# A batch of layer 3 moved ahead of a folding, and the last unit of a scan summed part by part

## The chip, the cores and the metric

The kernel runs on one core of one Trainium2 chip. The metric is the device time of one execution in microseconds (us). The five engines run their own instruction queues side by side: PE (matrix products, from SBUF into PSUM), DVE and POOL (elementwise work), ACT (functions and copies) and SP, which here issues the DMAs.

## The reference

Four layers run one after the other over 8 images of 192 channels and 64 x 64 pixels, all in f32.

- Layer 0: normalisation, a gate branch, a 3x3 depthwise convolution, then a selective scan in four directions, normalised, gated, weighted by channel and added to the input.
- Layer 1: a mixing layer with no recurrence.
- Layer 2: a selective scan again, and a normalisation.
- Layer 3: windows of the image, in three layouts, go through a small attention and a 3x3 depthwise convolution, and are folded back.

The scan, with h a state of 16 values for each channel, and cut to its core:

```python
def step(h, inp):
    dt_t, B_t, C_t, x_t = inp
    h = h * jnp.exp(dt_t[..., None] * A[None]) + (dt_t * x_t)[..., None] * B_t[:, :, None, :]
    return (h, jnp.einsum('bkcn,bkn->bkc', h, C_t))
```

Layer 3, with the three layouts (number of windows along a side, step, window side): (4, 16, 16), (8, 8, 8) and (12, 5, 9). The windows of the third overlap:

```python
xc = _conv1x1(x, w1, b1)
for nw in WINDOWS:
    ...
    u4 = u3.reshape(-1, C, k, k)
    a = _se(_conv1x1(u4, w2, b2), wse1, wse2) + _dwconv3x3(u4, wpos, bpos)
    ...
    folded = jnp.zeros((N, C, H, W), xc.dtype).at[:, :, hidx, widx].add(p)
    out_list.append(folded / cnt[None, None, :, :])
out = _conv1x1(jnp.concatenate(out_list, axis=1) + x, w3, b3)
```

The `reshape` to `u4` mixes pixels and channels, so each batch passes through DRAM on its way in and out.

## The kernel before

For each image the program runs `scan_layer` (layer 0's scan), `layer0_out`, `layer1`, `put_sequences`, `scan_layer` again (layer 2's scan) and `between`. There are so 16 scan layers in an execution. `between` mixes two generators: `behind`, the rest of this image (end of layer 2, and layer 3), and `ahead`, the start of the next image. For the last image it holds `behind` alone.

**The scan.** A scan layer has 48 units: two directions, eight chunks of 512 positions, three groups of 128 channels. The order on every engine is written out by hand (`manual_schedule`): the loop over `k` is the unit, the loop over `j` its eight steps. A unit's state tile `da` is 128 partitions by 4 parts (`NB`) by 16 states (`NS`) by 128 positions (`SB`). Per unit:

- ACT writes the decay into `da` (L244). PE fills the input `u` (L287). DVE scans two times per part (L308).
- `times_c` multiplies each part by C on POOL (L319, 128x2048), as soon as its two scans are done, in the next step `j`. POOL then adds the last states onto others (L322), four of them in the first two parts and three in the other two, so that 12 (or 13) states are left.
- `add_up` sums the states on PE, with matmuls by the identity that accumulate in the PSUM tile `py`: one matmul of 512 columns for each of 12 states over all four parts (L337), and one of 256 columns for the 13th state of the last two (L342). They are queued in the list `to_add` at step 2 of the next unit and drawn off a few at a time.
- `finish` adds the sum to the rest in `yo` on DVE (L352, L356) and stores it (L357). `load_y` loads, in the second direction, what the first one left (L328).

The loop runs for two turns beyond the last unit, so that its sum and its `finish` have a place. The pools of the next stage take the scan's memory when its last store has landed.

**Layer 3.** `behind` works on four batches of windows: two halves of the third layout (`first`, `second`), the first layout (`third`) and the second (`fourth`). `gates` loads a batch (L897), sets it into a padded tile and works out the gate. `convolve` makes the 3x3 taps in groups (six for each half of the third layout, four for each of the others). In a group PE makes four taps (L939), ACT one (L951), POOL the gated input (L945) and its sum with ACT's tap (L954), DVE the last four (L957) and the sum of all (L960). At the end the batch is stored to DRAM (L966). `move_windows` loads a layout back (L860): the third layout `p2` into tile `t1`, later the first two, `p01`, into the same tile `t1`.

Folding adds windows onto the image: the third layout on DVE (one half of the partitions, ten ops) and POOL (the other half, eight ops) at L991, after the accumulator was zeroed on POOL (L985), then two scalings of the overlaps on DVE (L999, L1002); the first two layouts on DVE and POOL in turn (L1011). The output follows (L1020 to L1028).

In `between` the order in which the program is written gives the priorities, but the order on each engine is drawn up by a planner when the program is built, so instructions can pass others that aren't ready.

Of the kernel before, what the change touches and what calls it, by code (L numbers as in the profile page):

```python
# [9 lines left out]
ALU = mybir.AluOpType  # L10
# [11 lines left out]
NS = 16  # L22
SB = 128
NB = Q // SB
# [16 lines left out]
def tile_net(ctx: ExitStack, tc: tile.TileContext, a: dict, out: bass.AP):  # L41
    nc = tc.nc
# [5 lines left out]
    ident = cst.tile([P, P], F32, name="ident")  # L48
# [50 lines left out]
    def scan_layer():  # L99
# [5 lines left out]
        with (  # L105
# [13 lines left out]
            NP = 12  # L119
            units = [  # L120
                (d, i, i if d == 0 else nck - 1 - i, v)
                for d in range(2) for i in range(nck) for v in range(3)
            ]
            vt, xd, cdr, dg = {}, {}, {}, {}
            dts, dtx, dtt, das, cts, us, py, yo = {}, {}, {}, {}, {}, {}, {}, {}

# [189 lines left out]

            def times_c(k, g):
                h = das[k][:, NB - 1 - g if units[k][0] else g]
                nc.gpsimd.tensor_tensor(h, h, cts.pop((k, g)), ALU.mult)  # L319
                n = NS - NP if g < 2 else NS - NP - 1  # L320
                to = h[:, NP - n : NP]
                nc.gpsimd.tensor_tensor(to, to, h[:, NS - n : NS], ALU.add)  # L322
# [9 lines left out]
            def add_up(count):  # L332

                for k, n in to_add[:count]:
                    if n == 0:
                        py[k] = sp.tile([P, Q], F32, tag="py", name="py")
                    nc.tensor.matmul(  # L337
                        py[k], ident, das[k][:, :, n, :], start=(n == 0), stop=(n == NP - 1)
                    )
                    if n == 8:  # L340
                        s = slice(0, NB // 2) if units[k][0] else slice(NB // 2, NB)
                        nc.tensor.matmul(  # L342
                            py[k][:, s.start * SB : s.stop * SB], ident, das[k][:, s, NP, :],
                            start=False, stop=False,
                        )
                del to_add[:count]

            def finish(k):
                d, i, c, v = units[k]
                p, y = py.pop(k), yo.pop(k)  # L350
                if d == 0:
                    nc.vector.scalar_tensor_tensor(  # L352
                        y, vt[k // 3][:, v, :], skip[:, v : v + 1], p, ALU.mult, ALU.add
                    )
                else:
                    nc.vector.tensor_tensor(y, y, p, ALU.add)  # L356
                nc.sync.dma_start(out=(ys if d else yp)[v][:, c * Q : (c + 1) * Q], in_=y)  # L357

            nu, nm = len(units), len(units) // 3


            SUM = ((1, 0, 1, 2, 0, 2, 1, 2), (2, 2, 1, 1, 1, 2, 2, 2), (2, 1, 1, 2, 2, 2, 2, 2))
# [2 lines left out]
            def has(k):  # L365
                return 0 <= k < nu
# [24 lines left out]
                    fill(0, 0)  # L391
            for r in range(2):
                diagonals_b(0, 1, r)
            for k in range(nu + 2):
                m, v = divmod(k, 3)
                ahead = 0 <= m + 1 < nm
                for j in range(8):
                    if v == 1 and j == 3 and 0 <= m + 2 < nm:
                        load_v(m + 2)
                    if has(k):  # L400
                        scan(k, j)
                    if j == 7:
                        if has(k + 1):
                            cut(k + 1)
                        if has(k):
                            keep(k)
                    if j % 2 == 0:
                        kk, g = (k, j // 2 - 1) if j else (k - 1, 3)
                        if has(kk):
                            times_c(kk, g)  # L410
                        if has((4 * kk + g + 3) // 4):
                            load_c(*divmod(4 * kk + g + 3, 4))
                    if j == 5 and has(k + 2):
                        steps_c(k + 2)
                    kk, jj = (k, j + 1) if j < 7 else (k + 1, 0)
                    if has(kk):
                        fill(kk, jj)
                    if j == 2:
                        if has(k - 2):
                            finish(k - 2)  # L420
                        if has(k - 1):
                            load_y(k - 1)
                        if has(k + 1):
                            turn(k + 1)
                    if ahead and (v, j) == (0, 4):

                        steps_a(k + 3)
                        steps_a(k + 4)
                    if ahead and v == 1 and j == 1:

                        steps_b(k + 2)
                        steps_a(k + 4)
                        steps_b(k + 3)
                        steps_b(k + 4)
                    if v == 0 and ahead:
                        if j == 0:
                            project_a(m + 1)
                        if j == 1:
                            project_b(m + 1)
                    if v > 0 and ahead:  # L440
                        if j == (5, 1)[v - 1]:
                            diagonals_a(m + 1, v - 1)
                        if j >= 6:
                            diagonals_b(m + 1, v - 1, j - 6)
                    if j == 2 and has(k - 1):
                        to_add += [(k - 1, n) for n in range(NP)]
                    add_up(SUM[v][j])
                    if has(k + 1) and j in DECAY:
                        decay(k + 1, *DECAY[j])

# [343 lines left out]
    def behind(b, pool, wk, psp, table):  # L794
# [55 lines left out]
        def move_windows(i, t, dram, store):  # L850
            if i < 2:
                pairs = [(t[half(i)], dram[i])]
            else:
                pairs = [(t[half(0)], dram[2][:, 0 : 45 * 144])]
                pairs += [(t[half(1)][:, 0 : 36 * 144], dram[2][:, 45 * 144 :])]
            for s, d in pairs:
                if store:
                    nc.sync.dma_start(out=d, in_=s)
                else:
                    nc.sync.dma_start(out=s, in_=d)  # L860
# [71 lines left out]
        def convolve(k, kk, mh, per, u4, pad, gate, to):  # L932
            for g in range(0, mh, per):
                ms = slice(g, g + per)
                ps = wide_("pw")[:, 0]
                tap = [divmod(t, 3) for t in range(9)]
                tap = [pad[:, g // per, dy : dy + k, dx : dx + k, :] for dy, dx in tap]
                for t in range(PE_TAPS):
                    nc.tensor.matmul(  # L939
                        ps[:, : per * kk], taps[:, t, :], tap[t],  # L940
                        start=(t == 0), stop=(t == PE_TAPS - 1),
                    )
                acc = wk.tile([P, Q], F32, tag="acc", name="acc")[:, : per * kk]
                turned = u4[:, ms, :].rearrange("p m j -> p j m")
                nc.gpsimd.tensor_tensor(  # L945
                    acc.rearrange("p (j m) -> p j m", m=per), turned,
                    gate[:, ms].unsqueeze(1).to_broadcast([P, kk, per]), ALU.mult,
                )
                tap = [t.rearrange("p r q m -> p r (q m)") for t in tap]
                term = wk.tile([P, Q], F32, tag="term", name="term")[:, : per * kk]  # L950
                nc.scalar.mul(  # L951
                    term.rearrange("p (r x) -> p r x", r=k), tap[PE_TAPS], pos[:, PE_TAPS : PE_TAPS + 1]
                )
                nc.gpsimd.tensor_tensor(acc, acc, term, ALU.add)  # L954
                rows = ps[:, : per * kk].rearrange("p (r x) -> p r x", r=k)
                for t in range(PE_TAPS + 1, 9):
                    nc.vector.scalar_tensor_tensor(  # L957
                        rows, tap[t], pos[:, t : t + 1], rows, ALU.mult, ALU.add
                    )
                nc.vector.scalar_tensor_tensor(  # L960
                    turned, ps[:, : per * kk].rearrange("p (j m) -> p j m", m=per), bpos,
                    acc.rearrange("p (j m) -> p j m", m=per), ALU.add, ALU.add,
                )
                yield "conv"
            for h, (af, m0) in enumerate(to):
                nc.sync.dma_start(out=af[:, m0 : m0 + mh, :], in_=u4[half(h)])  # L966
# [12 lines left out]
        fourth = gates(1, 0, 1, "t0", "t3")  # L979
        yield "gates"  # L980
        yield from convolve(*third)


        acc = room("t2", size["t2"])[:, 0:T]
# [16 lines left out]
        both = both.rearrange("p h (g r) -> p h g r", r=s)[:, :, :, 0 : k - s]  # L1001
        nc.vector.tensor_scalar_mul(both, both, 0.5)  # L1002
        p01 = room("t1", size["t1"])[:, 0:T]
        move_windows(0, p01, a3, False)
        yield from convolve(*fourth)
        move_windows(1, p01, a3, False)
        for i in range(2):
            nw, s, k = WINDOWS[i]
            for ki in range(k):
# [318 lines left out]
```

## Time and profile before

| | us |
|---|---|
| median of 3 runs | 25658.43 |
| lowest and highest | 25636.73, 25665.45 |
| the profiled execution | 25655.22 |
| its span | 25653.4 |

| engine | busy us | share of the span | instructions |
|---|---|---|---|
| PE (matmul) | 23083.9 | 90% | 173960 |
| DVE | 20611.1 | 80% | 21237 |
| POOL | 19165.2 | 75% | 7452 |
| ACT | 14171.8 | 55% | 23120 |

The mean granted clock of PE was 0.938 of full speed. "Busy" is an average over stages that have different limits. What counts for a change in one stage is what ends last there, so the shares above say little by themselves: the chain of waits and the timeline of the stage do. Times in those views are microseconds from the start of the span; "x7" means seven instructions merged into one row, and "[2.28 <-POOL da L319]" that the engine stood idle 2.28 us until POOL's instruction of line 319 was done.

### The profile page before, as it was taken

The page shows a single profiled execution, that of the slowest core. Times are in us where ns is not written, and L with a number is a line of the kernel's source. Part 1 is how long each engine was busy: PE and PEld are TensorE (multiplying, and loading weights), DVE is VectorE, ACT ScalarE, POOL GpSimd, SP SyncE. Part 2 cuts the span into 40 slices and gives each one's busy share as a digit, 9 for nine tenths or more (in the row PEclk, how much of TensorE's full clock was granted, in tenths as well). Part 3 has the DMA queues.
Part 4 walks back from the last instruction along what each step waited for, and adds up shares of the span by engine and source line. Part 5 has one row for each costly group of instructions (what it writes and reads, how often), then busy time and mean ns, then how long its engine had stood idle before and what let it go on. Part 6 is the DMA issues. An engine that isn't in the chain of part 4 may idle for free.

```text
span 25653.4 us, 431230 instructions
## 1 busy us (share of the span) xinstructions
PE 23083.9 (90%) x173960; PEld 12032.7 (47%) x173960; DVE 20611.1 (80%) x21237; ACT 14171.8 (55%) x23120; POOL 19165.2 (75%) x7452
## 2 busy tenths in 40 slices
PE   9989889898898988989889898898989989799896
PEld 4535345353453534535345353453535535355452
DVE  7969789697896968969689696886968879688795
ACT  5646456464564645646456464555645556455563
POOL 7939589395893958939589395894958949589495
PEclk9989999899998999989999899998999989899898
DMA  5636556365563655636556365563656646566364
GB/s 168 207 115 203 144 174 206 115 202 144 172 206 115 204 145 170 206 116 203 142 174 206 115 203 140 178 202 120 204 134 181 200 122 204 132 186 202 118 204 115
DMA packets 1204797, 4293.85 MB, mean 167 GB/s; under 512 B 360224, under 2 KB 419456, under 8 KB 804480
## 3 DMA queue, kind: packets, MB, share of 16 engines
q1 hardware_dynamic: 1202816, 4266.25, 56.5%
q8 instruction: 1388, 22.74, 0.4%
q14 instruction: 593, 4.86, 0.1%
HBM read 3810.55 MB, written 450.72 MB: 166 GB/s over the span
## 4 chain that ended last, share of the span: by engine, by line
POOL 37%; PE 12%; DVE 7%; ACT 3%; issue 3%; DMA 2%; SPq 0%; POOLq 0%; DVEq 0%; ACTq 0%
POOL da L319 28%; POOL da L322 6%; PE py L337 3%; POOL dtx L221 2%; PE u L287 2%; DVE da L308 2%; PE pa L501 1%; ACT da L244 1%; DVE pwc L957 1%; PE pa L504 1%; DVE t L991 1%; DMA a<-t 1%; DMA t<-u 0%; PE paa L501 0%; PE pac L501 0%
## 5 line engine op out<-in xcount | busy, mean ns | idle before, releaser
L308 DVE TENSOR_TENSOR_SCAN da<-da,u 128x1024 f32<-128x1024 f32 x6144 | 14041.7, 2286 | 324.1 <-ACT da L254 37.4
L319 POOL TENSOR_TENSOR da<-da,ct 128x2048 f32<-128x2048 f32 x3072 | 13925.0, 4533 | 330.7 <-DVE tmp L303 309.2
L337 PE MATMUL py<-da,ident 128*128 128x512 f32 x18432 | 9491.8, 627 | 542.2 <-POOL da L319 442.9
L287 PEld LDWEIGHTS u<-dg,dtt 32*128 32x128 f32 x131072 | 5942.5, 163 | 4597.8 <-issue 4309.1
L244 ACT ACTIVATE da<-dt,neg_a 128x512 f32<-128x512 f32 (+1 forms) x12544 | 7662.8, 699 | 16.3
L287 PE MATMUL u<-dg,dtt 32*128 32x128 f32 x131072 | 7232.6, 283 | 115.6 <-DVE da L308 48.6
L337 PEld LDWEIGHTS py<-da,ident 128*128 128x128 f32 x18432 | 3120.3, 191 | 3144.0 <-issue 2226.5
L322 POOL TENSOR_TENSOR da<-da 128x512 f32<-128x512 f32 (+1 forms) x3072 | 3484.2, 1134 | 240.9
L221 POOL TENSOR_TENSOR dtx<-dt,vt 128x512 f32<-128x512 f32 x768 | 978.2, 1275 | 3311.3 <-ACT dt L217 3245.6
L231 ACT COPY dtt<-misc 128x512 f32<-128x512 f32 x768 | 449.4, 585 | 3336.9 <-PE misc L229 3336.9
L305 DVE TENSOR_TENSOR u<-u,tmp 128x8 f32<-128x8 f32 x5952 | 1009.0, 170 | 1089.2 <-PE u L287 867.1
L234 ACT COPY dtt<-misc 32x512 f32<-32x512 f32 x3008 | 1732.2, 576 | 45.4
L196 DVE TENSOR_TENSOR dg<-msk,misc 128x1024 f32<-128x1024 f32 x1024 | 1222.9, 1197 | 440.1 <-DMA vt<-vs 277.8
L160 ACT ACTIVATE xd<-misc,msk 128x512 f32<-128x512 f32 x256 | 175.6, 686 | 1789.9 <-PE misc L156 1789.9
L217 ACT ACTIVATE dt<-misc 128x512 f32<-128x512 f32 x768 | 430.7, 595 | 1104.1 <-PE misc L213 1095.2
L945 POOL TENSOR_TENSOR acc<-u,gate 128x486 f32<-128x486 f32 (+1 forms) x80 | 108.3, 1358 | 966.7 <-DVE u L960 690.7
L939 PE MATMUL pwc<-t,l3taps 128*128 128x486 f32 (+1 forms) x1280 | 598.5, 617 | 233.4 <-DVE t L960 213.4
L901 POOL MEMSET t<- 128x4356 f32 (+2 forms) x32 | 100.3, 3135 | 936.9 <-DVE t L875 914.5
L229 PE MATMUL misc<-ident,dtx 128*128 128x128 f32 x3072 | 595.4, 318 | 0.0
L186 PE MATMUL misc<-ident,xd 16*128 16x16 f32 x4096 | 565.5, 266 | 25.6 <-DVE dg L196 25.6
L186 PEld LDWEIGHTS misc<-ident,xd 16*128 16x128 f32 x4096 | 528.1, 210 | 94.6 <-issue 93.1
L951 ACT ACTIVATE term<-t,l3p 128x486 f32<-128x486 f32 (+1 forms) x160 | 114.1, 713 | 826.4 <-POOL acc L954 826.4
(286 smaller groups left out, 18279.6 us busy)
## 6 DMA issues: line engine op xcount, KB each, us to landing
ct<-cd SPq DMA_DIRECT2D x2048, 1024.0 KB
ct<-cd SPq DMA_DIRECT2D x2048, 512.0 KB
vt<-vs SPq DMA_DIRECT2D x768, 256.0 KB
yp<-yo SPq DMA_DIRECT2D x384, 256.0 KB
yo<-yp SPq DMA_DIRECT2D x384, 256.0 KB
ys<-yo SPq DMA_DIRECT2D x384, 256.0 KB
yt<-ys SPq DMA_DIRECT2D x96, 512.0 KB
t<-ys SPq DMA_DIRECT2D x96, 512.0 KB
```

The costliest lines, as they stand in the source:

```text
L186: nc.tensor.transpose(pt[:, i * NS : (i + 1) * NS], xd[m][rows, cols], ident[rows, rows])
L196: nc.vector.tensor_tensor(dg[m, o][:, at], msk[:, 0:32].unsqueeze(1).unsqueeze(1).to_broadcast(shape), bts[m, o][:, at, r * 8 : r * 8 + 8] ...
L221: nc.gpsimd.tensor_tensor(dtx[k], dts[k], vt[k // 3][:, units[k][3], :], ALU.mult)
L234: (nc.scalar.copy if k else nc.vector.tensor_copy)(dtt[k][q * 32 : (q + 1) * 32, 1], pt[r * 32 : (r + 1) * 32])
L244: nc.scalar.activation(das[k][:, s, n, :], dts[k].rearrange("p (s t) -> p s t", t=SB)[:, s], AF.Exp, scale=neg_a[:, v, d, n : n + 1],)
L287: nc.tensor.matmul(u[ch, r * 4 : r * 4 + 4, e::4], dtt[k][rows, r, e, ch], dg[k // 3, o][rows, r * 4 + e, n], start=True, stop=True,)
L305: nc.vector.tensor_tensor(head, head, tmps[k][:, n], ALU.add)
L308: nc.vector.tensor_tensor_scan(h, h, u.rearrange("p n t -> p (n t)")[:, way], 0.0, ALU.mult, ALU.add)
L319: nc.gpsimd.tensor_tensor(h, h, cts.pop((k, g)), ALU.mult)
L322: nc.gpsimd.tensor_tensor(to, to, h[:, NS - n : NS], ALU.add)
L337: nc.tensor.matmul(py[k], ident, das[k][:, :, n, :], start=(n == 0), stop=(n == NP - 1))
L939: nc.tensor.matmul(ps[:, : per * kk], taps[:, t, :], tap[t], start=(t == 0), stop=(t == PE_TAPS - 1),)
```

## The change

Two things change.

In layer 3, `convolve(*fourth)` stands right behind `convolve(*third)`, ahead of the folding of the third layout. Before, it stood behind that folding and behind the load of the first layout. Both loads of `p01` now stand together after the folding and the two scalings.

In the scan, the last unit of a layer (`k == nu - 1`) is treated apart. Its last product by C is split over states: 0 to 7 on POOL, 8 to 15 on DVE, and POOL's addition of states is left out there. Its sum isn't made by `to_add` but by `add_last`: the first two parts together in 12 matmuls of 256 columns, placed ahead of the last product, then the third part in 13 and the fourth in 16 matmuls of 128 columns. The sum goes to a tile of the tag `misc` instead of `py`. Its `load_y` stands earlier (step 3 of its own turn), its `finish` follows that of the unit before, and the loop has one turn less.

```diff
+            nu, nm = len(units), len(units) // 3
...
             def times_c(k, g):
                 h = das[k][:, NB - 1 - g if units[k][0] else g]
+                if k == nu - 1 and g == NB - 1:
+
+                    ct = cts.pop((k, g))
+                    for eng, n in ((nc.gpsimd, slice(0, 8)), (nc.vector, slice(8, NS))):
+                        eng.tensor_tensor(h[:, n], h[:, n], ct[:, n], ALU.mult)
+                    return
                 nc.gpsimd.tensor_tensor(h, h, cts.pop((k, g)), ALU.mult)
...
+            def add_last(g0, g1):
+
+                k = nu - 1
+                if k not in py:
+                    py[k] = misc()
+                s = slice(NB - g1, NB - g0)
+                ns = NS if g1 == NB else NP + (g0 == 2)
+                for n in range(ns):
+                    nc.tensor.matmul(
+                        py[k][:, s.start * SB : s.stop * SB], ident, das[k][:, s, n, :],
+                        start=(n == 0), stop=(n == ns - 1),
+                    )
...
-            for k in range(nu + 2):
+            for k in range(nu + 1):
...
                         if has(k - 2):
                             finish(k - 2)
-                        if has(k - 1):
+                        if k == nu:
+                            finish(k - 1)
+                        if has(k - 1) and k < nu:
                             load_y(k - 1)
...
-                    if j == 2 and has(k - 1):
+                    if (k, j) == (nu - 1, 3):
+                        load_y(k)
+                    if j == 2 and has(k - 1) and k < nu:
                         to_add += [(k - 1, n) for n in range(NP)]
                     add_up(SUM[v][j])
+                    if (k, j) == (nu - 1, 7):
+                        add_last(0, 2)
+                    if (k, j) == (nu, 0):
+                        add_up(NP)
+                        add_last(2, 3)
+                        add_last(3, 4)
...
         yield from convolve(*third)
+        yield from convolve(*fourth)
...
         p01 = room("t1", size["t1"])[:, 0:T]
-        move_windows(0, p01, a3, False)
-        yield from convolve(*fourth)
-        move_windows(1, p01, a3, False)
+        for i in range(2):
+            move_windows(i, p01, a3, False)
```

More of the change, by code (lines that the diff above doesn't have):

```diff
@@ L357, in finish @@
                 nc.sync.dma_start(out=(ys if d else yp)[v][:, c * Q : (c + 1) * Q], in_=y)
-            nu, nm = len(units), len(units) // 3
             SUM = ((1, 0, 1, 2, 0, 2, 1, 2), (2, 2, 1, 1, 1, 2, 2, 2), (2, 1, 1, 2, 2, 2, 2, 2))
```

## The prediction

> **What bounds the kernel now.** I read the page's chain of work first: it says which engines end the work.
>
> ```profile
> POOL 37%; PE 12%; DVE 7%; ACT 3%; issue 3%; DMA 2%; SPq 0%; POOLq 0%; DVEq 0%; ACTq 0%
> POOL da L319 28%; POOL da L322 6%; PE py L337 3%; POOL dtx L221 2%; PE u L287 2%; DVE da L308 2%; PE pa L501 1%; ACT da L244 1%; DVE pwc L957 1%; PE pa L504 1%; DVE t L991 1%; DMA a<-t 1%; DMA t<-u 0%; PE paa L501 0%; PE pac L501 0%
> ```
>
> The steady scan hangs on POOL's product by C (L319). The change leaves that alone and touches two stretches where POOL doesn't rule: the end of each of the 16 scan layers, and layer 3 of each of the 8 images. So I took each stretch by itself, in image 3 (counted from 0). First the timeline of a scan's end:
>
> ```profile
> 12417.69 0.56 PEld L229 LDWEIGHTS misc<-ident,dtx 128*128 128x128 f32 x4
> 12417.69 0.75 PE L229 MATMUL misc<-ident,dtx 128*128 128x128 f32 x4
> ...
> 12461.81 0.59 PE L342 MATMUL py<-da,ident 128*128 128x256 f32 x2
> 12462.25 2.74 PE L337 MATMUL py<-da,ident 128*128 128x512 f32 x6
> 12462.71 4.51 POOL L319 TENSOR_TENSOR da<-da,ct 128x2048 f32<-128x2048 f32 x1 [1.59 <-DVE da L308]
> 12467.27 7.99 PE L337 MATMUL py<-da,ident 128*128 128x512 f32 x18 [2.28 <-POOL da L319]
> 12478.30 0.69 DVE L356 TENSOR_TENSOR yo<-yo,py 128x512 f32<-128x512 f32 x1 [12.59 <-PE py L337]
> 12479.02 0.32 SPq L357 DMA_DIRECT2D ys<-yo  x1
> ```
>
> To be seen: PE finishes unit 46, stands still 2.28 us for the last product of unit 47, and only then makes all of that unit's sum. One sum matmul is two PE instructions of 0.43 us at 512 columns and 0.215 us at 256 (the two of L342: 12461.81 to 12462.25). The sum is 12.5 matmuls, 10.75 us. The next stage starts when the store of 12479.02 has landed.
>
> Then the chain of waits through layer 3:
>
> ```profile
> 12841.85 16.66 DVE t L991 x7
> ...
> 12887.57 1.15 DVE t L960
> ...
> 12889.39 6.92 DMA a<-t
> ...
> 12896.38 8.86 DMA t<-a
> ...
> 12905.37 8.90 POOL xa L1011 x4
> ...
> 12914.31 3.78 PE pac L501 x4
> ```
>
> To be seen: the third layout's folding (L991), then the fourth batch's taps (L957, ending in L960), then that batch goes to DRAM (6.92) and comes back as a layout (8.86), and 8.90 of folding (L1011) stand between it and the output. The two DMAs cover nothing. L991 to L1011 takes 63.1 to 63.7 us in all five images that I looked up.
>
> Last the groups, kept apart by shape:
>
> ```profile
> L991 DVE TENSOR_TENSOR t<-t,t 64x720 f32<-64x720 f32 x40 | 114.4, 2920 | 0.0
> L991 DVE TENSOR_TENSOR t<-t,t 64x576 f32<-64x576 f32 x40 | 98.4, 2517 | 0.0
> L1011 POOL TENSOR_TENSOR xa<-xa,t 64x512 f32<-64x512 f32 x32 | 71.1, 2268 | 132.3 <-DMA t<-a 132.3
> ```
>
> To be seen: with both engines folding, a DVE op of 720 columns takes 2.92 us and one of 576 takes 2.52.
>
> **Layer 3, step by step.** The move takes nothing away: it puts four groups of taps (DVE 4 x 0.76 + 1.11 = 4.18 us a group, from L960 12825.33 to 12829.50), their POOL and ACT work and the two stores ahead of the folding, and puts both loads of the small layouts behind it.
>
> Taps: the first group's four L957 already run ahead of the folding today (12838.82 to 12841.85), so the order within this stage is drawn up by a planner, and it may mix again. With the taps first, one L960 and three groups remain after 12841.85: 1.1 + 3 x 4.18 = 13.7, to 12855.6. PE needs 3.7 us a group (12834.93, eight instructions), POOL 2.8 (1.5 + 1.3), so DVE sets the pace. The store then runs under the folding, and costs nothing as long as 7 us of folding follow (without that cover 7.5 us an image, as today).
>
> Folding: today 10 ops on DVE and 8 on POOL, side by side, 26.7 us (12841.85 to 12868.64). The DVE op that ran with no L991 of POOL beside it took 1.29 us, against 2.5 and 2.9; L957, which reads PSUM, takes 0.73 to 0.75 beside POOL's L1011 and 0.75 without. So folding against folding costs double, folding beside taps nothing. I take 1.35 us a DVE op alone, hence (26.7 - 13.5) / 8 = 1.6 for POOL's. The accumulator's memset on POOL (3.51, L985) ran at 12837.87 and I leave it there, in a gap of POOL's. POOL is through with the taps 4 us before DVE and folds 2.6 ops in that time; 5.4 ops at 2.86 beside DVE take it to 12871, when DVE has done 5.5 of ten; 4.5 x 1.35 more end it at 12877. Bounds: 12869 if POOL folds all its part under the taps (13.5 after 12855.6), 12882 if it folds none of it (26.7, also the case if the memset comes last).
>
> The Trainium skill, "SBUF — State Buffer" (its section on the port that VectorE and GpSimd share), says that a DVE op with two SBUF inputs and a POOL op that reads SBUF lock each other out for a whole instruction. The 1.29 against 2.9 agrees; by that rule POOL's early ops would be free, by a plain sharing of bandwidth at all times the folding would end at 12882.
>
> Loads: both layouts go into the tile that holds the third layout, so they wait for the last L991. One lands after 8.7 (12868.70 to 12877.37); the second, even if wholly behind it, lands before the first is folded. The two scalings (2.36 + 1.78, L999 and L1002) fall under the load instead of between taps. Small foldings: 16 ops of 64x256 (POOL 8 x 1.06 = 8.5 to 9.1, today hidden among taps) and 8 of 64x512 (8.9): 18 us, now all exposed. End: 12877 + 8.8 + 18 = 12904, against 12914.3: 10 us saved. With the bounds above it is 5 (12882 + 8.8 + 18.2) to 19 (12869 + 8.7 + 17.4). Eight images: 80 us, 40 to 150. SP's queue: ahead of the loads stand the eight stores of `ev` (done by about 12870, since their tiles now come free under the taps); behind them the next scan's `vt` loads, which are not used before 12941.
>
> **The scan's end.** Added on PE: 12 matmuls of 256 columns (24 x 0.215 = 5.16 us), 13 and 16 of 128 columns: 58 instructions. Removed: 10.75. The first 24 need products done at 12451.8, so they start as unit 46's n=10 ends and fill PE's gap. What follows needs the third group (folded at 12461.1) and the last product, by then long done: half of it on POOL is 2.3 us, the DVE half (128x1024) about 1.2 like L530's 1.22, even one after the other 3.5, and PE comes to it only some 9 us after n=10. That POOL's L322 (1.0) falls away costs three narrow matmuls, counted above. Behind PE's wait stands unit 46's n=11: its finish on DVE slips from 12465 to 12470, with only the last finish behind it on that queue. The load of `yo` moves to an earlier place on SP, behind the store of unit 45; nothing waits there. The dropped turn of the loop issues nothing.
>
> The open price is a 128-column PE instruction with a 128x128 weight load of its own. No row shows it in a sum; the nearest is L229: four loads in 0.56, a first of 0.20 and steps of 0.12. By columns alone it is 0.107 (half of 0.215); the weight load's full length, 0.19 (L337's and L342's groups), is the far end. I take 0.12: 58 x 0.12 = 6.96. Saving per tail = PE's idle + what a low clock adds + 10.75 - 5.16 - 6.96. Idle over all 16 tails: twelve of 2.28, three of 3.97, one of 3.78: 43.1. In six tails the 18 instructions took longer than 7.99 (9.39, 9.69 three times, 11.03, 11.04; granted clock 0.78 to 0.88 in the three that I looked up), 12.6 us together; without the gap I expect full clock. 43.1 + 12.6 - 16 x 1.37 = 34 us saved; 46 at 0.107, and 31 lost at 0.19.
>
> The Trainium skill's "TensorE: Matmul & The Clock Gate" (Part 2, back-to-back issue gap) has pairs of weight load and 128-column matmul at 81 ns where the matmul alone takes 56. In that ratio, an estimate, the narrow ones would take 0.155 and this part would save 1 us.
>
> **Sum.** 80 + 34 = 114. The profiled execution took 25655.2 (span 25653.4), the median shown is 3.2 above it: 25655.2 - 114 + 3 = 25544.
>
> **Rivals.**
> A, the move has little effect: the planner, which mixes taps and folding already, keeps much of the folding on DVE before the last taps, or the folding gets no cover, while the narrow matmuls cost 0.15 to 0.19. For it: L957 at 12838.82 out of order. Against: the taps' inputs are ready at 12839. Layer 3 saves 40, the tails between +6 and -31: 25612 to 25649, within 0.2%.
> B, slower: narrow weight loads don't hide. Place: the 58 instructions of each tail. If load and stream add up, 0.19 + 0.107 = 0.30, or each waits for the one before, 0.39 (one L229 matmul by itself), the sum needs 17 to 23 us instead of 7: 16 x 10.4 = 167 to 250 lost against the forecast, 25710 to 25795. It cancels the whole gain from 0.243 on (114 / 928 instructions above 0.12). Against: L337's and L342's loads lie under the running matmuls (0.215 at 256 columns, with a load of 0.19).
> The Trainium skill's same page (Part 3, what overlaps) lets a load overlap a running matmul only in other row groups, which would be B; the 0.215 of L342 contradicts it.
> C, something else in the mixed stage (SP's or POOL's order) gives the gain back: no row to price it.
>
> **Chances.** Forecast 0.70 (own range 25495 to 25607), A 0.15, B 0.07, C 0.08. Range 25495 to 25655: it takes in A and the bounds, without layer 3's extreme of 150. About 0.2% (51 us) is what a measurement here can tell from no change: faster 0.70, same 0.15, slower 0.15.
>
> **What would show it.** In the tails: no idle of PE before the last sum, 58 instructions in 7 us, store to store about 7 instead of 13.3 us. In layer 3: L960 of the fourth batch by 12856 in this image's time, the store under L991, both t<-a together after the last L991, L1011 ending 10 us earlier. I am wrong if the narrow matmuls pass 0.25 us, or if DVE or POOL stand idle between taps and folding.

## The result, and the profile after

The changed kernel takes 25586.33 us (median of 9 runs, 25570.56 to 25602.87); the kernel before took 25648.41 beside it (9 runs, 25631.13 to 25665.45). The ratio is 0.9975, with a 95% interval of 0.9965 to 0.9986: faster by 62 us of the 114 forecast, inside the range. The profiled span went from 25653.4 to 25584.6, by 68.8. Two places hold it, within a microsecond (69.3):

| stretch, summed over the execution | before | after | saved | forecast |
|---|---|---|---|---|
| 16 tails: end of a scan layer's last DVE scan to end of its last `finish` | 281.0 | 235.8 | 45.2 | 34 |
| 8 times layer 3: end of the third batch's taps to end of the last small folding on POOL | 594.4 | 570.3 | 24.1 | 80 |

From the page's chain of work, shares of the span by engine:

```profile
POOL 36%; PE 13%; DVE 5%; ACT 4%; issue 3%; DMA 2%; SPq 0%; POOLq 0%; DVEq 0%; ACTq 0%
```

POOL still leads. DVE went from 7% to 5%. Before, the third layout's folding stood under DVE (L991, 1%); in image 3's chain below it stands under POOL (L1021).

**The tail.** The timeline of image 3's first scan's end (start, duration, engine, line, and in brackets the idle time before the group with what ended it). L344 is the old sum, L363 the sum by parts, L324 the split product, L376 the finish:

```profile
12424.07 2.35 POOL L324 TENSOR_TENSOR da<-da,ct 128x1024 f32<-128x1024 f32 x1
12424.15 3.35 DVE L324 TENSOR_TENSOR da<-da,ct 128x1024 f32<-128x1024 f32 x1
12425.45 5.34 PE L363 MATMUL misc<-da,ident 128*128 128x256 f32 x24
12430.63 1.02 PE L344 MATMUL py<-da,ident 128*128 128x512 f32 x2
12431.48 6.64 PE L363 MATMUL misc<-da,ident 128*128 128x128 f32 x58
12438.16 0.69 DVE L376 TENSOR_TENSOR yo<-yo,misc 128x512 f32<-128x512 f32 x1 [5.79 <-PE misc L363]
```

PE's gap is gone: none of its groups has an idle time in brackets, the 24 instructions of 256 columns start while the last product is being made, and the 58 narrow ones take 6.64 us, against 7 forecast. All 16 tails now take 14.74 us, with a granted clock of 1.00 in each sum; before they took from 16.36 to 21.10, and in the six slow ones the sum ran at 0.78 to 0.88.

**Layer 3.** The chain of waits in image 3, whose third batch ends at 12796.18 (the name behind an engine is the tile it made; SPq is SP's queue, DMA a transfer):

```profile
12817.37 5.21 POOL t L1021 x3
...
12824.03 1.84 POOL t L1021
12825.96 1.50 POOL acc L974
12827.52 1.27 POOL acc L983
12828.82 0.59 ACT ev L1186
12829.46 1.08 PE pcola L1180 x4
...
12838.28 0.46 SPq L889
12838.83 0.60 SPq L995
12839.49 10.40 DMA a<-t
12849.96 9.75 DMA t<-a
12859.84 8.92 POOL xa L1040 x4
12868.81 3.78 PE pac L530 x4
```

The store of the fourth batch (`a<-t`) and the load behind it (`t<-a`) still stand one after the other on the path, as they did before, and 8.92 us of folding behind them. Ahead of the taps' last POOL work (L974, L983) stands POOL's folding (L1021). And there is a name in the chain that has nothing to do with the two edits: `ev`. It belongs to `put_columns`, the tail of the *next* image's layer-0 preparation, which is planned into the same stretch.

The groups of the foldings, by shape (busy us and mean ns; idle before):

```profile
L1021 DVE TENSOR_TENSOR t<-t,t 64x720 f32<-64x720 f32 x40 | 72.7, 1822 | 0.0
L1021 DVE TENSOR_TENSOR t<-t,t 64x576 f32<-64x576 f32 x40 | 64.3, 1612 | 0.0
L1040 POOL TENSOR_TENSOR xa<-xa,t 64x512 f32<-64x512 f32 x32 | 71.1, 2274 | 32.1 <-DMA t<-a 32.1
```

The mixing with taps made the DVE foldings cheaper, as forecast: 1.82 us where it was 2.92, 1.61 where it was 2.52. That is (2.92 - 1.82 + 2.52 - 1.61) x 5 = 10 us less of DVE's work an image; only 3 us an image reached the end.

Where they went is told by each queue's own order in this stretch. PE, ACT, DVE and SP, from their timelines:

```profile
12802.42 3.67 PE L968 MATMUL pwc<-t,l3taps 128*128 128x512 f32 x8 [2.43 <-DVE t L989]
12817.33 0.58 ACT L1186 COPY ev<-pcola 64x512 f32<-64x512 f32 x1 [11.29 <-POOL acc L983]
12817.96 1.12 PE L1180 MATMUL pcola<-hb,ident 64*64 64x256 f32 x4 [11.86 <-ACT ev L1186]
12820.89 1.12 PE L1180 MATMUL pcola<-hb,ident 64*64 64x256 f32 x4 [1.81 <-ACT ev L1186]
12821.93 5.12 PE L968 MATMUL pwc<-t,l3taps 128*128 128x512 f32 x8
12827.09 0.76 DVE L986 SCALAR_TENSOR_TENSOR pwc<-t,l3p,pwc 128x512 f32<-128x512 f32 x1 [7.57 <-PE pwc L968]
12817.93 19.19 SPq L1190 DMA_DIRECT2D vs<-ev  x7
12837.86 0.33 SPq L140 DMA_DIRECT2D vt<-vs  x1
12838.28 0.46 SPq L889 DMA_DIRECT2D t<-a  x1
12838.83 7.19 SPq L995 DMA_DIRECT2D a<-t  x2
```

On PE, two groups of `put_columns` (L1180) stand ahead of the fourth batch's last taps (L968). PE stood idle 11.86 us for ACT's copy `ev`, which itself had waited 11.29 us for POOL's L983, and the taps stood behind; DVE then waited 7.57 us for those taps. On SP, seven stores of `ev` took 19.19 us, and a `vt` load followed, ahead of the load and the store of layer 3. The third layout's folding had ended at 12833.55, so its tile was free 4.7 us before the load was issued.

Against the forecast, in us from the third batch's end in image 3:

| | before | forecast | after |
|---|---|---|---|
| third layout folded | 29.7 | 38 | 37.4 |
| fourth batch's last L960 (now L989) | 49.7 | 16.6 | 40.7 |
| last small folding on POOL | 75.3 | 65 | 72.6 |

### The profile page after: what moved, and what is told of

Same layout as the page of the kernel before. It is cut to its first block, busy times and chain, and to the rows that moved or that the text cites. A ratio compares the mean times of both kernels' runs of the same rounds, so it can differ in the third digit from the quotient of the medians.

```text
span 25584.6 us, 433060 instructions
## 1 busy us (share of the span) xinstructions
PE 23083.5 (90%) x174856; PEld 12129.3 (47%) x174856; DVE 20590.3 (80%) x21253; ACT 14175.8 (55%) x23120; POOL 19097.7 (75%) x7436
## 4 chain that ended last, share of the span: by engine, by line
POOL 36%; PE 13%; DVE 5%; ACT 4%; issue 3%; DMA 2%; SPq 0%; POOLq 0%; DVEq 0%; ACTq 0%
POOL da L326 27%; POOL da L329 6%; PE py L344 3%; PE u L288 2%; POOL dtx L222 2%; DVE da L309 2%; PE pa L530 1%; ACT da L245 1%; PE pa L533 1%; DMA a<-t 1%; PE misc L363 1%; DVE pwc L986 0%; DMA t<-u 0%; PE paa L530 0%; PE pac L530 0%
## 5 line engine op out<-in xcount | busy, mean ns | idle before, releaser
L344 PE MATMUL py<-da,ident 128*128 128x512 f32 x18048 | 9304.0, 627 | 504.0 <-POOL da L326 407.0
L344 PEld LDWEIGHTS py<-da,ident 128*128 128x128 f32 x18048 | 3043.1, 191 | 2998.5 <-issue 2134.8
L974 POOL TENSOR_TENSOR acc<-u,gate 128x486 f32<-128x486 f32 (+1 forms) x80 | 108.5, 1360 | 962.0 <-DVE u L989 688.8
L968 PE MATMUL pwc<-t,l3taps 128*128 128x486 f32 (+1 forms) x1280 | 590.7, 610 | 40.2 <-DVE t L989 20.1
L986 DVE SCALAR_TENSOR_TENSOR pwc<-t,l3p,pwc 128x486 f32<-128x486 f32 (+1 forms) x640 | 467.0, 736 | 136.6 <-PE pwc L968 123.8
```

The source lines that it names most:

```text
L344: nc.tensor.matmul(py[k], ident, das[k][:, :, n, :], start=(n == 0), stop=(n == NP - 1))
```

## The experiments

Three questions: whether the two parts add up; what in layer 3 holds the fourth batch back to 40.7; and what sets the tail.

**One part alone.** e1 keeps the tail's part and puts the taps back behind the first scaling and load; e2 is the kernel before with the taps moved alone.

```diff
 # e1: the changed kernel
-        yield from convolve(*third)
-        yield from convolve(*fourth)
+        yield from convolve(*third)
...
-        for i in range(2):
-            move_windows(i, p01, a3, False)
+        move_windows(0, p01, a3, False)
+        yield from convolve(*fourth)
+        move_windows(1, p01, a3, False)
```

> The scan's part of the change alone; layer 3 as before. From the two traces the 16 tails (end of the last scan to the end of the last finish on DVE) took 281.0 us before and 235.8 after. Theory (the saved time passes straight on, since the next stage starts at the landing of the last store): 45 us less than before, 16 tails of 14.74. Rival (the next stage takes some of it back, or the tails differ from trace to trace because of the granted clock): under 25 us less.

> Layer 3's part of the change alone; the scan as before. Theory: 24 us less than before (3 us an image, from 75.3 to 72.4 between the end of the third batch and the end of the last folding). Rival (the two parts work on each other): the gain is another, and the two parts' gains do not add up to the change's 62 to 69.

e1 took 25615.2 us (11 runs), ratio to the kernel before 0.9983 [0.9975, 0.9992]; its tails sum to 235.76, its layer 3 to 600.3, which is 6 more than in the profile of before with the same code. That is 34 us where 45 were expected; the interval, 21 to 64, takes in both. e2 took 25624.05 (11 runs), ratio 0.9989 [0.9980, 0.9997]; tails 280.5, layer 3 569.5, the fourth batch at 40.6. Within the noise the parts add up: 34 and 25 us against 62 together. The stretches are the firmer measure, since the rest of a profile varies without an edit touching it: e2's span is 29 us shorter than its two stretches explain. The move alone shows the same 40.6, so the tail's part has no share in what went missing in layer 3.

**What holds the fourth batch: `ev`'s tiles.** `ev` and the taps' `term` share two buffers of one tag (the tiles of a tag take turns in its buffers). A copy into `ev` waits until a `term` is read by POOL (L983) or an older `ev` has been stored, and PE and SP queue up behind it. e3 gives `ev` the buffers of another tag; e4 does that to the kernel before.

```diff
-            ev = wk.tile([P, Q], F32, tag="term", name="ev")
+            ev = wk.tile([P, Q], F32, tag="stab", name="ev")
```

> The change, and in put_columns the copy ev takes its tile from the tag stab (two tiles that are free by then) instead of term, which the taps use. Theory Q (queues): in the change the matmuls of put_columns stand on PE ahead of the fourth batch's last group and wait for a term tile that POOL frees late, and the stores of ev stand on SP ahead of the load and the store of layer 3. With tiles of their own they are done before the taps: fourth batch ready by 26 us after the end of the third instead of 40.6, last folding over at 64 to 67 instead of 72.4, 6 to 8 us an image in the seven images that have put_columns, 40 to 55 us less than the change. Theory M (mixing): the fourth batch is late because its taps are mixed with the folding on DVE and POOL; then ev's tiles change nothing: 40 and 72, the same time as the change.

> The kernel before with ev in the tag stab, and nothing of the change. Theory Q: in the old order the fourth batch waits for the folding whatever put_columns does, so 0 to 2 us an image, 0 to 15 us less than before. Rival (ev's place costs as much in either order): 40 us or more less than before.

e3 took 25529.29 us (5 runs, 25510.65 to 25549.63), ratio 0.9951 [0.9938, 0.9965]: 57 us below the changed kernel. Layer 3 sums to 492.9, some 61.3 in each of the seven images that have `put_columns`. Its chain of waits in image 3, whose third batch ends at 12775.20:

```profile
12805.08 2.54 POOL t L1021
12807.70 2.80 POOL acc L974
12810.57 1.27 POOL acc L983
12811.86 1.10 DVE t L989
12813.63 6.59 DMA a<-t
12820.27 7.23 DMA t<-a
12827.63 8.90 POOL xa L1040 x4
```

`ev` has left the chain, and the transfers take 6.59 and 7.23 instead of 10.40 and 9.75. The total is what the theory of the queues asked for, and more. But the fourth batch ends at 37.7, not by 26 as expected: on POOL the last folding op (12805.08) stands ahead of that batch's last L974 and L983. So there is a second order behind the first. It costs little here, because SP is free: the first load was issued at 12807.65, as POOL's last folding op ended (12807.62), and lies beside the taps and the store.

e4 took 25642.44 (11 runs), ratio 0.9996 [0.9987, 1.0004]; layer 3 summed to 584.0 in its profile, 10 less than before. By its time the same edit can't be told from nothing, as expected. With the taps where they were, the shared tag costs 10 us at most by these profiles, and e1's 600.3 beside 594.4 shows how far two profiles of one code can lie apart; where the taps are moved it costs 57. The tails, whose code e4 doesn't touch either, sum to 269.7 in its profile: the low clock of before comes and goes, so the tails' part is worth some 34 to 45 us by the profile that is taken.

**PE's order alone.** e5 keeps the shared tag, and lets no L1180 be queued ahead of the last tap matmul (`issue_after` keeps an instruction behind another on its queue).

```diff
+                    marks["pw"] = nc.tensor.matmul(   # the last of the taps
...
+            with ExitStack() as late:
+                if "pw" in marks:
+                    late.enter_context(tc.issue_after(marks["pw"].ins))
                 for g in range(2):
                     nc.tensor.matmul(
```

> The change, with the matmuls of put_columns (pcola) held on PE behind the fourth batch's last tap matmul; ev keeps its tiles of the tag term. Theory Q (PE's and SP's queues): DVE's 7.6 us of waiting for PE's last taps is gone, the fourth batch is ready by 33 us after the end of the third instead of 40.6; the stores of ev still stand on SP ahead of the load, so the last folding is over at 66 to 69 (72.4 in the change, 61.3 with tiles of ev's own). Theory M (mixing on DVE and POOL alone): fourth batch at 37 or later and 71 or more.

One run, 25555.46 us, beside 25639.08 for the kernel before. Layer 3 sums to 549.5, 68.8 to 70.0 in the seven images; in image 3 the folding ends at 32.4, the fourth batch at 37.7 and the last small folding at 69.7. That is just past the 66 to 69 of the theory of the queues, and the fourth batch's place is the one of the theory of mixing (37 or later): both have a share. With PE's wait gone the batch stands where it stands in e3, behind POOL's folding. SP's timeline shows what of the loss is left:

```profile
12808.84 19.04 SPq L1195 DMA_DIRECT2D vs<-ev  x4
12828.05 0.46 SPq L889 DMA_DIRECT2D t<-a  x1
12828.61 6.97 SPq L995 DMA_DIRECT2D a<-t  x2
```

The stores of `ev` still take 19.04 us and the load comes behind them. So PE's order is worth 570.3 to 549.5. The rest, down to 492.9 in e3, where `ev` is early enough to free SP as well, lies by this timeline with SP.

**The order that the prediction assumed.** e6 is e5 with the third layout's folding held behind the fourth batch's last op on each engine.

```diff
+                with tc.issue_after(marks["pool" if h else "dve"].ins):
                     (nc.gpsimd if h else nc.vector).tensor_tensor(
                         to, to, view(p2[half(h)], 2, 5)[:, ki - 5 * h, kj0:kj1], ALU.add
                     )
```

> As the run before, and the third layout's folding is held behind the fourth batch's taps on DVE and on POOL: the order that the prediction's sum assumed. By that sum: fourth batch ready 17 us after the end of the third, folding over at 38, both loads together, last folding over at 65. Rival (the mixed order of the change is the better one, since the folding is over earlier than 38 there when nothing stalls, and the first layout's load with it): 65 or more, behind the 61.3 of the run with ev's own tiles.

One run, 25543.3 us. Layer 3 sums to 500.25, 94.1 less than before. The chain of waits in image 3 (third batch's end at 12795.78; folding is L1022 here, the small foldings L1041), and SP's part of it:

```profile
12812.33 20.59 DVE t L1022 x9
12832.94 1.21 DVE t L1022
12834.21 7.52 DMA t<-a
12841.79 8.51 POOL xa L1041 x8
12850.36 8.74 POOL xa L1041 x4
```

```profile
12813.74 2.52 SPq L995 DMA_DIRECT2D a<-t  x2
12834.21 1.13 SPq L889 DMA_DIRECT2D t<-a  x2
```

This is the picture that the prediction drew: the fourth batch at 16.75, its store at 12813.74 under the folding, the folding's end at 38.4 (12834.15), both loads issued together right behind it, one transfer of 7.52 on the path, then 8.51 and 8.74 of small foldings. The end is at 63.3, where the forecast had 65. Inside the folding the two engines shared the time otherwise than forecast:

```profile
12807.13 14.89 POOL L1022 TENSOR_TENSOR t<-t,t 64x720 f32<-64x720 f32 x8
12812.33 21.80 DVE L1022 TENSOR_TENSOR t<-t,t 64x720 f32<-64x720 f32 x10
```

POOL ran its eight ops in one go, 1.80 to 2.26 us each. DVE's first op lasted 11.0 us, until POOL was through, and its other nine took 1.15 to 1.43 each. In the kernel before, the two took turns op by op. The sum is nearly the same: in these rows, either way, an op of one engine stands still while the other's runs.

The run's 25543.3 us lies next to the forecast's 25544 by luck: the two stretches save 139 us together in its profile, and its span is only 112 us shorter, the rest of the profile being longer.

**SP's order alone, by another queue.** e11 is the changed kernel with the stores of `ev` issued on ACT's queue.

```diff
-            nc.sync.dma_start(out=vs[2][up, c * Q : (c + 1) * Q], in_=ev[up])
+            nc.scalar.dma_start(out=vs[2][up, c * Q : (c + 1) * Q], in_=ev[up])
```

> The change with the eight stores of ev issued from ACT's queue instead of SP's; the matmuls of put_columns stay where they are on PE. This takes away SP's share alone. Theory (two shares): the fourth batch is late as in the change (40 us), but the first layout's load goes out at the end of the folding (37.3 instead of 42.1) and the store at 40.7 instead of 42.7, so the last folding is over 2 to 4 us earlier, 68 to 70 instead of 72.4. Rival (SP's stores are no bound): 72.

One run, 25575.75 us; layer 3 sums to 563.4, 71.1 in image 3, where 68 to 70 were expected. A miss: 6.9 us over the eight images. SP's timeline tells why (third batch's end 12804.83):

```profile
12846.19 0.33 SPq L140 DMA_DIRECT2D vt<-vs  x1
12846.62 0.48 SPq L889 DMA_DIRECT2D t<-a  x1
```

Without the stores, SP still has the next scan's first `vt` load ahead of layer 3's load, and that one reads what the stores of `ev` write. Moving the stores to another queue moves the wait into the `vt` load. So SP's share isn't shown by itself here; what e3 shows is that it goes when `ev` comes early.

**What sets the tail.** e7 lets POOL add the fourth (last) part's last states too, so that parts three and four are summed together and the sum has 26 instructions of 256 columns in the place of 58 of 128; e8 also makes the product whole again on POOL.

```diff
 # e7; e8 has the first two lines replaced by the third
-                    for eng, n in ((nc.gpsimd, slice(0, 8)), (nc.vector, slice(8, NS))):
-                        eng.tensor_tensor(h[:, n], h[:, n], ct[:, n], ALU.mult)
+                    nc.gpsimd.tensor_tensor(h, h, ct, ALU.mult)     # e8 alone
+                    to = h[:, 9:12]
+                    nc.gpsimd.tensor_tensor(to, to, h[:, 13:16], ALU.add)
...
-                ns = NS if g1 == NB else NP + (g0 == 2)
+                ns = NP + (g0 == 2)
...
-                        add_last(2, 3)
-                        add_last(3, 4)
+                        add_last(2, 4)
```

> The change, with the third and fourth part of the last unit summed together in 13 matmuls of 256 columns instead of 13 and 16 of 128; POOL adds the last part's states 13 to 15 onto 9 to 11 after its half of the split product. Theory P (PE alone sets the tail now): 26 x 0.215 = 5.6 us instead of 58 x 0.112 = 6.5, tails of 13.85 instead of 14.74 us. Rival (the product or POOL's addition ends last): 14.7 or more, and PE waits for POOL before the last sum.

> As the run before, with the last product whole on POOL again, so without the split of the change. Theory P: the product is over 4.5 us after the last scan and the addition 1 us later, still before PE comes to it (6.5 us after the end of the last scan), so the tails are 13.85 us too, and the split on two engines gives nothing. Rival (the split is what shortens the tail): 15 us or more.

One run each: 25579.33 and 25583.33 us, too few to rank them by time. The tails say it: 13.87 us each in both (sums 221.96 and 221.97), against 14.74. The timeline of e8's same tail (product L323, addition L325, sum L364):

```profile
12425.60 4.50 POOL L323 TENSOR_TENSOR da<-da,ct 128x2048 f32<-128x2048 f32 x1
12426.81 5.34 PE L364 MATMUL misc<-da,ident 128*128 128x256 f32 x24
12430.19 1.00 POOL L325 TENSOR_TENSOR da<-da 128x384 f32<-128x384 f32 x1
12432.85 5.78 PE L364 MATMUL misc<-da,ident 128*128 128x256 f32 x26
```

The whole product of 4.50 and the addition of 1.00 end at 12431.19, 1.7 us before PE comes to that part. With the sum in this order the split on two engines buys nothing.

**Both mends together.** e9 is e8 with `ev` on its own tag; e10 is e9 with the folding held as in e6.

> The change with ev in tiles of its own (as e3) and the tail's sum in 12 and 13 matmuls of 256 columns with the product whole on POOL (as e8). The two parts lie in different stages, so their gains should add: 16 x 0.87 = 14 us less than e3's 25529, so 25515, tails of 13.87 and last folding over at 61.3. Rival (part of either gain is given back in a later stage): 25529 or more.

> As e9, and the third layout's folding is held behind the fourth batch's taps on DVE and POOL (as e6). With put_columns out of the way the strict order has fourth batch 16.7, folding 37 to 38, last folding over at 62 to 63 after the end of the third, against 61.3 for the mixed order in seven images, and 60.8 against 63.6 in the last one: the same time as e9 within 10 us. Rival (the order matters as long as it is not the one with put_columns in between): more than 15 us from e9.

e9 took 25509.47 us (5 runs, 25508.64 to 25527.23), ratio to the kernel before 0.9948 [0.9935, 0.9962]; its tails sum to 222.0, its layer 3 to 493.75. e10 took 25516.0 (25498.24 to 25545.62), ratio 0.9948 [0.9935, 0.9960]; 222.0 and 505.7. The gains of e3 and e8 add up. e9 and e10 can't be told apart by time, though layer 3 is 12 us longer in e10's profile: with `ev` out of the way, holding the folding back gives nothing. e9 beats the kernel before, and all its runs lie below all those of the changed kernel.

## Why the prediction was right, and where it was wrong

The sign and the range held. Both terms were off in size, in opposite directions: 34 forecast and 45.2 measured in the tails, 80 and 24.1 in layer 3. That the total lies inside even the forecast's own range is therefore partly luck: layer 3's 24.1 is below the 40 that was its lowest bound, and the tails came out near the upper end of theirs (46).

**The tails.** The mechanism was right in each step: PE's gap filled, the low clock gone, the narrow instructions near 0.12, the two stores 6.5 us apart where about 7 was forecast. A plain tail of before (16.36) became 14.74, 1.62 less, where the prediction's terms give 0.91 (2.28 + 10.75 - 5.16 - 6.96). Of the 0.71 between them, 0.28 is that the old sum took 11.03 from its first matmul to the finish (12467.27 to 12478.30) and not 10.75; 0.26 that the new one took 11.86 (12425.45 to 12438.16, less 0.85 for unit 46's L344 between) and not 12.12; 0.17 isn't traced. The low clock's share and that of the longer gaps was right: the tails of before held 19.2 us above 16 x 16.36, as the prediction's 12.6 and the longer gaps' 6.6 have it, and after they hold nothing. Rival B fell: 58 narrow instructions in 6.64 us are 0.114 each, far from 0.243.

**Layer 3's prices.** In sum they were right, and e6 shows it: in the order that the prediction assumed, 16.75, 38.4 and 63.3 stand against 16.6, 38 and 65, and 94 us are saved in layer 3 against 80. How the folding's time falls to the two engines was wrong (POOL's part ended at 26.2, not at 32), but not its sum.

**The step that failed** is the order itself, in two sentences of the prediction. "With the taps first" took it that moving four lines in the program moves them on every queue. On PE the planner put `put_columns` between them, on POOL the folding (e3 and e5: 37.7 with PE's wait gone; e6: 16.75 with POOL's order mended too). And "the eight stores of `ev` (done by about 12870, since their tiles now come free under the taps)": the stores stand ahead of the loads, as said, but they were not done. Their tiles came free late, since POOL's L983 stood behind POOL's folding; SP issued seven of them in the 19.19 us up to 12837.12, 41 us after the third batch's end where the forecast's 12870 is 31 in its own time, and past the folding's end at 12833.55. The two are one knot: taps wait on PE for `ev`, `ev` waits for a `term` that POOL frees only after foldings, and SP waits for `ev`. Of the signs that the prediction named for layer 3 none came, and the one that would prove it wrong did: DVE stood idle for 7.57 us between taps and folding.

So the store came back onto the path with 10.40 us, and 6 us of waiting ahead of it (12833.5 to 12839.49); of the 18 us of small foldings that the forecast had exposed, only 8.92 were, since the other half (from 12846.53 to 12855.05) ran beside the store and the second load. 37.4 + 6.0 + 10.4 + 9.8 + 8.9 make 72.5 of the 72.6; the rest are gaps between them.

What happened in layer 3 is therefore rival C (the order of SP and POOL), which had a chance of 0.08 and no price, with a part of A (the planner mixes; and 24 is less than the 40 that A left to layer 3). A's own cause, the mixing of taps and folding, is not what cost most of the time: in e3 the folding is still mixed with the taps, and layer 3 is 7 us shorter than in e6's clean order (in e9 12 us shorter than in e10).

What stays open: SP's share by itself, since e11 only moved its wait; and whether e9 or e10 is faster.

## What to carry to other kernels

Where a planner draws up the queues, moving lines in the program moves priorities and not instructions: before a gain is booked to an earlier place, list for each queue what of the *other* stage stands between, and what each of those waits for. A buffer tag shared by two stages ties their queues together; it can cost next to nothing (e4) until one of the stages is moved, and 57 us after that (e3). And when work on the last part of a sum is to be hidden, order the sum so that the parts already there go first, before dividing the last part among engines: without the split the tails were no longer than with it (e8 and e7, 13.87 us both).

## What the runs showed of the hardware that was not expected

- A PE instruction of 128 columns with a weight load of its own takes 0.114 us (106.2 us for 928 of them in the groups of L363), near half of the 0.215 of 256 columns; the record of a load lasts 0.191 there. So the loads nearly vanish under the stream and overlap one another, even though each is longer than the step from one instruction to the next. The Trainium skill's ratio ("TensorE: Matmul & The Clock Gate", Part 2) would have made it 0.155, an estimate, and is not seen here; nor is its Part 3's rule that only other row groups overlap.
- Both halves of the split product read and write SBUF, and one waits for the whole of the other. In six of the 16 tails POOL began first, by up to 0.09 us: its half took 2.34 or 2.35 us and DVE's 3.35 to 3.38. In six others DVE began first: its half took 1.22 or 1.23 and POOL's 3.33 to 3.35. The Trainium skill's "SBUF — State Buffer" ("Who interferes with whom") has such ops lock each other out for a whole instruction, and the trace agrees. Side by side, the halves took 3.43 us (12424.07 to 12427.50); POOL alone takes 4.50 for the whole.
- Which engine gets the next turn differs: in the kernel before, the foldings of DVE and POOL took turns op by op, and in e6, where POOL had begun first, DVE's first op lasted 11.0 us until POOL had done all of its eight. Why is open.
- With PE's gap closed, all 16 tails came within 0.01 us of one another. The spread of before, up to 4.75 us a tail, was the length of the gap (2.27 to 3.98 us) and the low clock behind it; two gaps of 2.27 us stood ahead of sums at 0.87, and gaps of 2.28 ahead of sums at 1.00, so the length alone doesn't tell.
